# A hybrid layer on one NeuronCore: work between the scans issued by a running account of engine times, in place of fixed credits

## The chip, the cores and the metric

The kernel runs on one core of one Trainium2 chip. The metric is the device time of one execution in microseconds, lower is better. Each engine of the core (PE for matmuls, DVE for vector work, ACT for activations, POOL for general elementwise work, SP for issuing DMAs) runs its own list of instructions in the order in which the program issued them; engines wait for each other through semaphores. PEld is the loading of weights on the PE.

## The reference, cut to what matters

The input is x of shape 4 x 1024 x 128 in float32. Four blocks follow each other, each with a residual:

```python
x = x + attention(layernorm(x))            # 16 heads of 8; a window of 32 and every 64th position
x = x + mlp(layernorm(x))                  # 128 -> 512 -> 512 -> 128, weights of +1 and -1
x = x + mamba(layernorm(x))                # see below; it adds its own residual as well
x = x + mlp(layernorm(x))
```

The change concerns the third block and the two MLPs beside it. The core of the third block, for E = 256 channels and N = 16 states per channel:

```python
u2 = silu(conv(u) + conv_b)                # depthwise, 4 taps
dt = softplus(dt_lo @ W_dt + b_dt)
def step(h, inp):                          # over the 1024 positions
    dA = exp(dt_t[..., None] * A)
    h = dA * h + (dt_t * u_t)[..., None] * B_t[:, None, :]
    y_t = einsum('ben,bn->be', h, C_t)
y = (y + u2 * D_param) * silu(z)
out = y @ W_out
```

## The kernel before, in words

**Stages.** Attention comes first, in a software pipeline of its own (lines 208 to 590), until about 250 us. Then the first MLP tiles and what the first scan needs are issued by turns until about 321 us. Then come the scans (`scans`, L1059), until about 884 us, with all the rest of the layer woven between them. A tail follows: the last part of the third block's output and its MLP.

**The scans.** A part is one batch element (4) and one half of the sequence (2 x 512 positions): 8 parts in a fixed order. A unit is one part and one of the 16 states: 128 units in order. Each unit i has these instructions, and the loop of `scans` writes their order out by hand:

- `drive(i + 2)`, POOL: `db` = `du` (dt times u2) times the row of B, which a DMA on SP's queue spreads over the partitions (`bs`, `load_b`). Three buffers of `db`.
- `decay(i + 1, h)`, ACT: `da` = exp(dt times A) for each half h of the channels. One tile `da` for each half, with two buffers in PSUM in all, so that `da` of the next unit can only be written when the scan of this unit has read its own.
- two scans, DVE: `hs` from `da` and `db`, one for each half of the channels, with `carry` as the start in the second half of the sequence; in the first half of the sequence ACT copies the last column to `carry`.
- `pcc`, PE: the row of C spread over the partitions by a matmul. One buffer: it can be written when the last unit's `hc` has read it.
- `hc`, DVE: `hs` times `pcc`. Six buffers, shared with some of the MLP's hidden tiles.
- `fold(i)`, POOL: adds `hc` of two neighbouring units, one half of the channels at a time. On POOL it stands ahead of `drive(i + 2)`, and on even i it waits for `hc` of unit i - 1.
- `total(i)`, PE: adds the folded `hc` into `pys` by a matmul with the identity. `gated(i)`, DVE: once in a part and half, `gate` times `pys`.

**The work between.** Everything else is a set of generators (`Work`, L625), which yield a `Piece` (L598) ahead of each small group of instructions: how many PSUM banks the group takes, how many microseconds it costs on which engine (`pe`, `ve`, `sc`, `gp`), whether it empties banks (`evict`), whether it is `urgent`, whether it is a `lump` (two activations with a table load on each side). The generators are: `mamba_pre_half` (L905) for each part (matmuls `pz`, `pc`, `px`, `pd`; activations `gate`, `u2`, `dt`; POOL `du`), `mamba_norm` (L850; `mxn`, `mxnT`, the statistics `rs_z` on POOL), `mamba_out` (L994; `pmo`), and two lanes of `mlp` (L682; `fxn`, `fxnT`, `pf`, `h1`, `pg`, `h2`, `pfo`). Three banks (`SPARE`, L1157) are for them all.

**What sets their order.** The loop of `scans` offers two places in each unit. At each, `evictions()` (L1170) issues every piece that empties banks, whatever it costs, save that lumps wait for the second place; then `pieces()` (L1180) gives each engine half of a fixed credit per unit (`RATES`, L1159: PE 2.9, DVE 1.2, ACT 2.4, POOL 1.2 us) and issues pieces until the credit is spent. The first place lies between `decay(i + 1, 0)` and `decay(i + 1, 1)`, so that what it puts on ACT stands between the two `da` of a unit. `ready` (L1200) issues pieces by force when a unit needs a part that isn't prepared. After the last scan the rest is issued in the order of the list, with `mamba_out_own(B - 1)` (L1020) put at its head.

Of the kernel before, what the change touches and what calls it, by code (L numbers as in the profile page):

```python
# [43 lines left out]
def hybrid_kernel(ctx: ExitStack, tc: tile.TileContext, x, Wq, Wk, Wv, Wo, ln_g, ln_b, W_in, conv_w,  # L44
# [108 lines left out]
    def ln_sums(src, name, soon=False):  # L153

        n = src.shape[1]
        st = small.tile([P, n, 6], F32, tag="st", name=f"st_{name}")
        mv = small.tile([P, n, 2], F32, tag="mv", name=f"mv_{name}")
        if among_scans[0] and not soon:

            for i in range(n):  # L160
                if i % 2 == 0:
                    yield Piece(sc=0.9)
                sc.activation(waste, src[:, i, :], AF.Identity, accum_out=mv[:, i, 0:1])
            yield Piece(gp=0.2)
            gp.tensor_scalar_mul(st[:, :, 0], mv[:, :, 0], -1.0 / C)
            yield Piece()
            for i in range(n):
                if i % 2 == 0:
                    yield Piece(sc=0.9)
                sc.activation(waste, src[:, i, :], AF.Square, bias=st[:, i, 0:1], accum_out=mv[:, i, 1:2])  # L170
            yield Piece(gp=0.2)
            gp.tensor_scalar_mul(mv, mv, 1.0 / C)
            return mv
        for i in range(n):
            if i % 2 == 0:
                yield Piece(ve=0.9)
            ve.bn_stats(st[:, i, :], src[:, i, :])
            ve.bn_aggr(mv[:, i, :], st[:, i, :])
        return mv
# [423 lines left out]


# [20 lines left out]
    class Work:  # L625


        def __init__(self, pieces):
            self.pieces = pieces
            self.held = 0  # L630
            self.next = next(pieces, None)

        def run(self):
            self.held = self.next.banks + (0 if self.next.evict else self.held)
            self.next = next(self.pieces, None)
# [46 lines left out]
    def mlp(u, tiles, split, pool, lane, own=None, soon=False, hasty=False, stats=None):  # L682
# [11 lines left out]
        def empty(dsts, srcs, relu):  # L694


            n = len(srcs)
            yield Piece(n if split else 0, evict=True, sc=0.6 * n, same=soon or hasty)
            for dst, bk in zip(dsts, srcs):
                if relu:  # L700
                    sc.activation(dst[:, 0], bk, AF.Relu)
                else:
                    sc.copy(dst[:, 0], bk)
            if split:
                yield evict(ve=0.7 * n)
                for dst, bk in zip(dsts, srcs):
                    high = dst[:, 0].bitcast(F32)
                    if relu:
                        ve.scalar_tensor_tensor(dst[:, 1], bk, 0.0, high, ALU.max, ALU.subtract)
                    else:  # L710
                        ve.tensor_sub(dst[:, 1], bk, high)
# [3 lines left out]
        yield Piece(sc=1.7)  # L715
        xn = fx.tile([P, nt, C], F32, name=f"fxn{u}", tag=f"fxn{lane}", bufs=1)
        ln_apply(xn, tiles, stats[:, 0], stats[:, 1])
        yield fill(1.2)
# [5 lines left out]
        for f0 in (0, 2):  # L724
            yield fill(1.0 if split else 1.8, 2, ready=(lambda: own or h1_free[0]) if f0 == 0 else None)
            if f0 == 0:
                if own:
                    h1 = own(u)
                else:
                    h1 = pool.tile([P, 4, 2, cols], kind, name=f"h1{u}", tag="h1")  # L730
                    h1 = [h1[:, f] for f in range(4)]
                    h1_free[0] = False
                h2 = pool.tile([P, 4, cols], F32, name=f"h2{u}", tag=f"h2{lane}")
            pf = [bank(f"pf{u}_{f0 + f}")[:, :cols] for f in range(2)]
            for f in range(2):
                w = wt(w0[:, (f0 + f) * P : (f0 + f + 1) * P])
                for s in range(parts):
                    te.matmul(pf[f], w, xnT[:, s], start=s == 0, stop=s == parts - 1)
            yield from empty(h1[f0 : f0 + 2], pf, True)
        for f0 in (0, 2):  # L740
            yield fill(2.0 if split else 1.8, 2)
            pg = [bank(f"pg{u}_{f0 + f}")[:, :cols] for f in range(2)]
            for f in range(2):
                for i in range(4):
                    if (i == 0 and f) or (i == 2 and not split):
                        yield more(2.0 if split else 1.8)
                    w = wt(w1[:, i, (f0 + f) * P : (f0 + f + 1) * P])
                    for s in range(parts):
                        te.matmul(pg[f], w, h1[i][:, s], start=i + s == 0, stop=i == 3 and s == parts - 1)
            yield evict(sc=1.2)  # L750
            for f in range(2):
                sc.activation(h2[:, f0 + f], pg[f], AF.Relu)
# [13 lines left out]
        yield evict(ve=0.75)  # L766
# [83 lines left out]
    def mamba_norm(bp, c):  # L850
# [10 lines left out]
        yield Piece(gp=2.2)  # L861
# [10 lines left out]
        yield Piece(sc=1.7)  # L872
# [9 lines left out]
        yield fill(1.2)  # L882
# [3 lines left out]
        yield Piece(sc=1.7, same=True)  # L886
# [18 lines left out]
    def mamba_pre_half(b, f):  # L905
# [16 lines left out]

        u2 = m2.tile([P, NH, CH], F32, name=f"u2{v}", tag="u2", bufs=3)
        for h in range(NH):
            for k in range(DC):
                if h + k == 0:
                    yield fill(1.8, 2, urgent=late)
                    pc = [bank(f"pc{v}_{h}") for h in range(NH)]
                elif k % 2 == 0:
                    yield Piece(pe=1.8, urgent=late)  # L930
                te.matmul(
                    pc[h], w_conv[:, k, h * P : (h + 1) * P], xnT[:, k : k + CH], start=k == 0, stop=k == DC - 1
                )
# [11 lines left out]
        yield fill(1.8, urgent=True)  # L945
# [7 lines left out]
        if not place:  # L953
# [3 lines left out]
            yield Piece(-1, urgent=True, sc=1.8)  # L957
# [17 lines left out]
        yield fill(1.8, 2, urgent=True)  # L975
# [18 lines left out]
    def mamba_out(bp, f):  # L994
# [3 lines left out]
        for q in range(HALF):  # L998
            yield fill(2.2)
            po = bank(f"pmo{bp}_{f}{q}")  # L1000
            for b2 in range(2):
                if b2:
                    yield more(2.2)
# [8 lines left out]
            yield evict(ve=0.75)  # L1012
# [7 lines left out]
    def mamba_out_own(b):  # L1020
# [6 lines left out]
        yield fill(1.7)  # L1027
        po = bank(f"pmo{b}_own")
        for g in range(4):
            if g == 2:  # L1030
                yield more(1.7)
# [27 lines left out]
    def scans(wide, ready):  # L1059
# [48 lines left out]
        def gated(i):  # L1108
# [3 lines left out]
            if not 0 <= k <= last:  # L1112
                return
            b, f, n = units[k]
            if n == N - 2:
                gate = mamba_pre[b, f][0]
                ve.tensor_mul(gate[:, h], gate[:, h], py.pop((b, f, h)))
                if h == NH - 1:
                    fed.add(("g", b, f))

        for i in range(3):
            load_b(i)
        for i in range(2):
            drive(i)
        for h in range(NH):
            decay(0, h)
        for i, (b, f, n) in enumerate(units):
            now[0] = i
            load_b(i + 3)
            fold(i)  # L1130
            drive(i + 2)
            pc = wide.tile([P, CH], F32, name=f"pcc{i}", tag="pcc")
            te.matmul(pc, spread[: 6 * N, n, :], mamba_pre[b, f][4], start=True, stop=True)
            hs = m2.tile([P, NH, CH], F32, name=f"hs{i}", tag="hs")
            db = dbs.pop(i)
            for h in range(NH):
                first = carry[b % 2][:, h, n : n + 1] if f else 0.0
                ve.tensor_tensor_scan(hs[:, h], das.pop((i, h)), db[:, h], first, ALU.mult, ALU.add)
            decay(i + 1, 0)
            evictions(lumps=False)  # L1140
            pieces()
# [3 lines left out]
            gated(i)  # L1145
            hss[i] = m2.tile([P, NH, CH], F32, name=f"hc{i}", tag="hc", bufs=6)
            ve.tensor_tensor(hss[i], hs, pc.unsqueeze(1).to_broadcast([P, NH, CH]), ALU.mult)
            total(i)
            evictions()
            pieces()  # L1150
# [6 lines left out]
    SPARE = 3  # L1157

    RATES = {"pe": 2.9, "ve": 1.2, "sc": 2.4, "gp": 1.2}  # L1159
    works = []  # L1160
    owed = dict.fromkeys(RATES, 0.0)

    def issue(w):
        for k, us in w.next.us.items():
            owed[k] -= us
        w.run()

    emptied = set()

    def evictions(lumps=True):  # L1170
        emptied.clear()
        for w in works:
            while w.next is not None and w.next.evict and (lumps or not w.next.lump):
                hasty = w.next.same
                issue(w)
                emptied.add(w)
                if w.held and not hasty:
                    break

    def pieces(forced=False):  # L1180


        for k, rate in RATES.items():
            owed[k] = min(max(owed[k], -2 * rate) + (0 if forced else rate / 2), rate / 2)
        left = SPARE - sum(w.held for w in works)
        for w in works:

            moved = w in emptied and now[0] < len(units) - 10
            while w.may() and not w.next.evict and w.next.banks <= left:
                if moved and not w.next.same and not (forced and w in emptied):  # L1190
                    break
                if not (forced or w.next.hurries()) and any(us and owed[k] <= 0 for k, us in w.next.us.items()):
                    break
                left -= w.next.banks
                issue(w)
                moved = True
            if forced and moved:
                break

    def ready(*part):  # L1200
        while part not in prepared:
            evictions()
            pieces(forced=True)
# [50 lines left out]
    with banks(SPARE), tc.tile_pool(name="wide", bufs=1, space=PSUM) as wide:  # L1254
# [12 lines left out]
        while any(w.next for w in works):  # L1267
            evictions()
            pieces(forced=True)
# [35 lines left out]
```

## Time and profile before

| what | us |
|---|---|
| median of 3 runs (lowest, highest) | 920.89 (917.93, 923.53) |
| the profiled execution's own time | 918.99 |
| its span, first to last instruction | 917.2 |
| first scan begins, last `hc` ends | 323.82, 884.47 |
| between these two: busy DVE, POOL, PE, ACT | 506.90, 507.93, 477.20, 406.60 |
| busy in the whole span: DVE, POOL, PE, ACT | 756.8, 747.2, 753.5, 592.3 |

The page's fifth part and the groups of instructions give for each kind its count, busy time, mean duration in ns and the idle time of its engine just before it, with what ended that. Nearly all instructions pass through one helper and so carry its line, L57: they are told apart by their tiles, which are named "out<-in". The waits give who waited for whom, in us, times and the longest. In the timeline a row starts with its start and its length in us. PEclk is the share of the full clock that was granted to the PE.

### The profile page before, as it was taken

The page shows a single profiled execution, that of the slowest core. Times are in us where ns is not written, and L with a number is a line of the kernel's source. Part 1 is how long each engine was busy: PE and PEld are TensorE (multiplying, and loading weights), DVE is VectorE, ACT ScalarE, POOL GpSimd, SP SyncE. Part 2 cuts the span into 40 slices and gives each one's busy share as a digit, 9 for nine tenths or more (in the row PEclk, how much of TensorE's full clock was granted, in tenths as well). Part 3 has the DMA queues.
Part 4 walks back from the last instruction along what each step waited for, and adds up shares of the span by engine and source line. Part 5 has one row for each costly group of instructions (what it writes and reads, how often), then busy time and mean ns, then how long its engine had stood idle before and what let it go on. Part 6 is the DMA issues. An engine that isn't in the chain of part 4 may idle for free.

```text
span 917.2 us, 15260 instructions
## 1 busy us (share of the span) xinstructions
PE 753.5 (82%) x5642; PEld 450.8 (49%) x5642; DVE 756.8 (83%) x1014; ACT 592.3 (65%) x1299; POOL 747.2 (81%) x580
## 2 busy tenths in 40 slices
PE   5797768875688978797789888969989889788897
PEld 2455435543466534442355444425455446455567
DVE  6699898999643279889799888897999999999862
ACT  4775537753345587889866777977777865654523
POOL 6699996999533188999988988999989999989730
PEclk9999769987589999897999997977999899899899
DMA  4633213330000121112111111211121222122001
GB/s 129 125 71 70 45 32 69 73 66 2 32 17 1 35 76 57 43 69 71 67 50 69 46 69 49 69 55 62 63 77 58 81 70 65 62 81 81 24 1 35
DMA packets 47163, 53.09 MB, mean 58 GB/s; under 512 B 4825, under 2 KB 38401, under 8 KB 47089
## 3 DMA queue, kind: packets, MB, share of 16 engines
q1 hardware_dynamic: 45920, 51.59, 19.9%
q8 instruction: 44, 0.72, 0.3%
q0 software_dynamic: 608, 0.27, 0.2%
q10 hardware_dynamic: 560, 0.26, 0.1%
q14 instruction: 31, 0.25, 0.1%
HBM read 45.82 MB, written 4.46 MB: 55 GB/s over the span
## 4 chain that ended last, share of the span: by engine, by line
DVE 32%; PE 26%; POOL 20%; ACT 12%; issue 8%; DMA 2%; SPq 0%; DVEq 0%; POOLq 0%; ACTq 0%
DVE hs L57 14%; POOL db L57 5%; DVE hc L57 5%; PE pga L57 4%; DVE S L57 4%; PE pys L57 4%; POOL prod L57 3%; POOL hc L57 3%; POOL prodv L57 3%; PE pc L57 3%; ACT da L57 2%; ACT L57 2%; PE pgb L57 2%; PE pfoa L57 2%; DVE or L57 2%
## 5 line engine op out<-in xcount | busy, mean ns | idle before, releaser
L57 POOL TENSOR_TENSOR db<-du,bs 128x1024 f32<-128x1024 f32 x128 | 302.6, 2365 | 0.7 <-DMA bs<-bd 0.7
L57 ACT ACTIVATE da<-dt,a_t 128x512 f32<-128x512 f32 x256 | 175.4, 687 | 127.2 <-DVE hs L57 126.6
L57 POOL TENSOR_TENSOR hc<-hc,hc 128x512 f32<-128x512 f32 x128 | 163.1, 1275 | 43.0 <-DVE hc L57 42.8
L57 DVE TENSOR_TENSOR hc<-hs,pcc 128x1024 f32<-128x1024 f32 x128 | 156.0, 1219 | 28.8 <-PE pcc L57 21.1
L57 DVE TENSOR_TENSOR_SCAN hs<-da,db 128x512 f32<-128x512 f32 x128 | 149.4, 1207 | 14.6 <-POOL db L57 7.3
L57 DVE TENSOR_TENSOR_SCAN hs<-da,carry,db 128x512 f32<-128x512 f32 x128 | 157.1, 1268 | 4.6 <-ACT da L57 4.6
L57 PE MATMUL pys<-hc,ident 128*128 128x512 f32 x256 | 147.1, 660 | 0.8 <-POOL hc L57 0.8
L57 PE MATMUL pcc<-bc,spread 96*128 96x512 bf16 x128 | 52.3, 409 | 35.7 <-DVE hc L57 34.8
L57 PEld LDWEIGHTS pys<-hc,ident 128*128 128x128 f32 x256 | 51.3, 210 | 51.7 <-issue 33.3
L57 PE MATMUL pga<-h1a,w 128*128 128x512 f32 x256 | 72.2, 431 | 2.5 <-ACT gate L57 1.8
L57 POOL TENSOR_TENSOR prod<-kv,qs 128x128 f32<-128x128 f32 (+14 forms) x30 | 71.0, 2368 | 3.2 <-DVE or L57 3.0
L57 POOL TENSOR_TENSOR prodv<-vS,E 128x128 f32<-128x128 f32 (+14 forms) x30 | 69.4, 2312 | 5.1 <-ACT E L57 4.8
L57 PE MATMUL pc<-mxnT,w_conv 128*128 128x512 f32 x128 | 61.8, 609 | 5.9 <-ACT gate L57 5.9
L57 ACT ACT_TABLE_LOAD x48 | 61.6, 1283 | 3.5 <-issue 2.6
L57 PEld LDWEIGHTS pga<-h1a,w 128*128 128x128 f32 x256 | 49.7, 197 | 27.8 <-issue 7.5
L57 PE MATMUL pgb<-h1b,w 128*128 128x512 f32 x192 | 59.0, 453 | 4.4 <-DVE fxnTc L57 3.1
L57 ACT ACTIVATE E<-S 128x512 f32<-128x512 f32 (+15 forms) x62 | 26.5, 473 | 52.1 <-DVE S L57 51.9
L57 PE MATMUL ps<-kx,qT 64*32 64x256 f32 x1008 | 46.8, 440 | 8.3 <-DVE S L57 5.8
L57 PEld LDWEIGHTS pgb<-h1b,w 128*128 128x128 f32 x192 | 38.2, 200 | 26.6 <-issue 7.4
L57 PE MATMUL py<-woT,oT 128*128 128x128 f32 x64 | 17.9, 368 | 39.0 <-ACT oT L57 38.7
L57 POOL TENSOR_TENSOR ep<-ep,eo 128x512 f32<-128x512 f32 x32 | 40.9, 1278 | 9.7 <-ACT ep L57 8.5
L57 ACT COPY ep<-pt 128x512 f32<-128x512 f32 x32 | 18.8, 586 | 38.8 <-DVE eo L57 36.1
(223 smaller groups left out, 1551.8 us busy)
## 6 DMA issues: line engine op xcount, KB each, us to landing
bs<-bd SPq DMA_DIRECT2D x64, 512.0 KB
vr<-vd SPq DMA_DIRECT2D x32, 256.0 KB
vd<-kv SPq DMA_DIRECT2D x8, 256.0 KB
x<-in_L_attn_a_x_dram SPq DMA_DIRECT2D x15, 128.0 KB
kx<-kT SPq DMA_DIRECT2D x104, 16.0 KB
out_dram<-x SPq DMA_DIRECT2D x12, 128.0 KB
taps<-in_L_attn_b_conv_w_dram SPq DMA_DIRECT2D x1, 512.0 KB
k1s<-in_L_ffn_k_dram SPq DMA_DIRECT2D x1, 256.0 KB
```

What stands on the lines that cost most here:

```text
L57: ins = getattr(self.engine, name)(*args, **kwargs)
```

## The change

Each engine gets a clock of the program's own (`times`), which `spend` moves on by a stated duration when an instruction is issued, starting no earlier than what it waits for. The loop of `scans` keeps it for its own instructions with durations written out in it. `ends` works out from it when a piece would be done, and whether the DVE would have to wait for it. At both places of a unit `pieces` issues whatever would be done by a deadline per engine, counted from the DVE's time; a piece in which the DVE would wait is held back. Pieces that empty banks are no longer exempt. The first place now lies after both `decay(i + 1, ·)`. Urgent is what a part needs that is 8 units away or less. The two lanes are taken in the order of which has issued fewer pieces. After the last scan, the piece that would be done first comes first. Stated durations are changed a little (ACT's statistics up, transposes from 1.2 to 0.65). The instructions themselves are the same.

```diff
-    RATES = {"pe": 2.9, "ve": 1.2, "sc": 2.4, "gp": 1.2}
+    times = dict(pe=0.0, ve=0.0, sc=0.0, gp=0.0)
...
+    def spend(engine, us, *others):
+        times[engine] = max(times[engine], *others, 0.0) + us
+        return times[engine]
+
+    def ends(w):
+        t, found, waits = w.since, {}, False
+        for k, us in w.next.us.items():
+            waits = waits or (k == "ve" and t > max(times[k], found.get(k, 0.0)) + 0.1)
+            t = found[k] = max(times[k], t) + us
+        return found, waits
...
+    def pieces(until=None):
+        for w in works[:-2] + sorted(works[-2:], key=lambda w: w.count):
+            moved = False
+            while w.may():
+                p = w.next
+                if not p.evict and p.banks > SPARE - sum(v.held for v in works):
+                    break
+                if until and p.us and (moved or not p.hurries()):
+                    found, waits = ends(w)
+                    spare_time = 0.8 if p.lump else 0.0
+                    if waits or any(t > until[k] + spare_time for k, t in found.items()):
+                        break
+                issue(w)
+                moved = moved or bool(p.us)
+                if not until:
+                    return
...
             decay(i + 1, 0)
-            evictions(lumps=False)
-            pieces()
             if f == 0:
                 sc.copy(carry[b % 2][:, :, n : n + 1], hs[:, :, CH - 1 :])
             decay(i + 1, 1)
-            gated(i)
+            t = times["ve"]
+            pieces(dict(pe=t + 2.0, ve=t + 1.5, sc=t + 4.2, gp=t + 6.2))
+            if gated(i):
+                spend("ve", 0.68, *after(("sum", i - 1)))
...
             total(i)
-            evictions()
-            pieces()
+            done["sum", i] = spend("pe", 0.9, *after(("fold", i - 1)))
+            t = times["ve"]
+            pieces(dict(pe=t + 1.7, ve=t + 1.5, sc=t + 3.0, gp=t + 5.0))
...
+        def hurry():
+            return now[0] >= place * PER - 8
...
         while any(w.next for w in works):
-            evictions()
-            pieces(forced=True)
+            able = [
+                w for w in works if w.may() and (w.next.evict or w.next.banks <= SPARE - sum(v.held for v in works))
+            ]
+            issue(min(able, key=lambda w: max(ends(w)[0].values(), default=w.since)))
```

## The prediction

> **What bounds the kernel now.** I read the stretch of the scans first (a table of busy times by stage), then the waits in it, then the timeline where waits are long.
>
> ```profile
> core 0: us, PE busy (x) PEld busy (x) DVE busy (x) ACT busy (x) POOL busy (x), PEclk, DMA share, GB/s
> 323.82:393.97 70.15, 56.45 (x196) 30.98 (x195) 62.41 (x70) 57.30 (x112) 63.38 (x47) 0.93 0.18 61
> 393.97:466.78 72.81, 57.21 (x145) 25.65 (x144) 61.27 (x59) 59.35 (x132) 68.23 (x55) 0.86 0.19 66
> ...
> 811.33:884.47 73.14, 61.88 (x248) 39.65 (x247) 68.42 (x72) 38.50 (x78) 56.38 (x40) 0.91 0.16 51
> sum 560.65, PE 477.20 PEld 265.52 DVE 506.90 ACT 406.60 POOL 507.93; mean PE 59.65 PEld 33.19 DVE 63.36 ACT 50.83 POOL 63.49
> ```
>
> Each row is one part of 16 units. The scans last 560.65 us, 4.38 a unit; DVE works 506.90 of it and POOL 507.93. Two engines are 90% busy, none is full. Which of them paces is told by the waits:
>
> ```profile
> engine line waited for: us in total, times, longest us
> ACT da L57 <- DVE hs L57: 126.6, 108, 4.0
> POOL hc L57 <- DVE hc L57: 37.9, 31, 4.0
> PE pcc L57 <- DVE hc L57: 34.8, 33, 3.1
> DVE hc L57 <- PE pcc L57: 21.1, 22, 3.5
> DVE hs L57 <- ACT da L57: 11.8, 11, 2.0
> DVE hs L57 <- POOL db L57: 7.3, 2, 7.0
> DVE fxnTa L57 <- ACT fxnTa L57: 5.1, 2, 2.7
> ```
>
> POOL, ACT and PE wait for the DVE. The DVE waits for PE's `pcc` 21.1 us, for `da` 11.8, and for POOL only 0.3 (the other 7.0 us are the start, ahead of the stretch). So DVE paces, and its idle time, 560.65 - 506.90 = 53.75 us, is what there is to win: `pcc` 21.1, `da` 11.8, `db` 0.3, its own evictions (`fxnT`, `h1`, `x`, nine kinds of wait together) 12.5, and 8.0 in gaps with no named releaser. A `da` wait as it looks on ACT:
>
> ```profile
> 621.61 0.69 ACT L57 ACTIVATE da<-dt,a_t 128x512 f32<-128x512 f32 x1
> 622.23 0.57 ACT L57 CAST bc<-px 32x512 bf16<-32x512 f32 x1
> 622.71 0.67 ACT L57 ACTIVATE da<-dt,a_t 128x512 f32<-128x512 f32 x1
> 623.33 1.63 ACT L57 ACTIVATE x<-x,rs_z 128x128 f32<-128x128 f32 x4
> 624.87 0.18 ACT L57 COPY carry<-hs 128x2 f32<-128x2 f32 x1
> 624.95 0.68 ACT L57 ACTIVATE da<-dt,a_t 128x512 f32<-128x512 f32 x1
> ```
>
> A `bc` and four `x` stand just ahead of the second `da` of a unit; so, too, did four `mxn` before 621.61, where the DVE lost 1.39 us.
>
> **What the Trainium skill says.** "Perfetto Trace Analysis", Optimization Strategy: take the most-contended engine, find the gaps between its slices and what blocks them; that is the way above, and this trace adds that of two equally busy engines the waits must choose. "TensorE: Matmul & The Clock Gate", Architectural detail: ACT and DVE are strict FIFO and PE only pulls weight loads ahead; the trace agrees, `da` waits behind `bc`. "ScalarE: Activation LUTs", What ACT_TABLE_LOAD costs: 1283 ns, and about 1380 of drain; the trace has 1283 for each of 48, and no such drain (load at 625.64, `dt` at 626.94).
>
> **The change, part by part**, by the order of instructions in the two built programs beside the durations above. The instructions are the same; all else is order.
>
> (1) *Both `da` first.* In the new order nothing stands between a unit's two `da` but the `carry` copy, which waits for the same scan as the second `da`. Extra ACT work comes behind them and can only delay the next unit's first `da`. From the end of a unit's scans, a lump there gives 0.70 + 0.18 for `da` and `carry`, 1.28 + 1.27 + 1.28 for the lump, 0.69 for the next `da`: 5.4 us. The DVE asks for it after `hc`, two scans, `hc`: 1.22 + 2.33 + 1.22 = 4.8. A lump costs 0.6 where the DVE has no extra work, and none where it has one (0.68 or more). There are 22 lumps (8 `gate`, 7 `u2`, 7 `dt`); I count about half: 6 us stay of 11.8. Bounds: 0 and 22 x 0.6 = 13.
>
> (2) *Deadlines for PE.* PE may be given work until 2.0 us past the scans, and 1.7 past `hc`; `pcc` (0.38) then has the next two scans (2.33) as cover. The cover fails where PE is slower than stated: eight `pga` matmuls are stated 1.9 and took 3.53 us at 565.59, with a granted clock of 0.70. The waits of 2.85 and 3.45 us lie in stretches at 0.70 and 0.68; these 6.3 stay, and one urgent `px` is put ahead of `pcc` 59: 7 us stay of 21.1. Bounds: 2 and 15.
>
> (3) *No eviction in which DVE would wait.* Held until the account says the data is there. Durations were nearly right, so 4 of 12.5 stay (1 to 8). Gaps of 8.0 stay.
>
> (4) *What is late next: POOL.* It has 507.93 us of work and its order is bound: fold, `db`. From the end of an `hc` it needs 1.27 + 2.36 = 3.6 us for `db`, while DVE asks for it after two units, 2 x 3.6 = 7.2: a slack of 3.6 us, which POOL can't widen, as the fold waits for `hc`. In quiet units DVE takes 2.33 + 1.22 = 3.55 and POOL 1.275 + 2.365 = 3.64, so a lag is made good only while DVE has extra work. The new order puts extras of 1.29 (`du`) to 2.7 us (`rs_z`) close together four times: near units 10 to 13, 40 to 44 (7.2 us in five units), 58 to 63, 68 to 71. At some 2 us beyond the slack each, the DVE now waits for `db`: 9 us in place of 0.3. This wait isn't in the trace of before; bounds 0 (the DVE's extras cover all) and 20 (POOL paces: 507.93 plus what it still waits). `du` of the fifth part now comes just ahead of `db` 64; its `dt` is done about 2.7 us after scan 61, its fold at 2.5, and `db` 64 at 7.7 where scan 64 asks at 8.5: nothing. On SP's queue the row of B for that part is written some units later than before, ahead of the same loads; `db` has waited for it only 0.7 us in all, and I count none.
>
> Sum: 7 + 6 + 4 + 8 + 9 = 34 idle in place of 53.75, a gain of 19.75. One DVE instruction more falls before the last `hc` (the last but one `x`, 0.75).
>
> (5) *The tail.* Before, after the last `hc`:
>
> ```profile
> 883.37 2.43 PE L57 MATMUL pgc<-h1c,w 128*128 128x512 f32 x8
> 885.64 2.74 PE L57 MATMUL pys<-hc,ident 128*128 128x512 f32 x6
> 888.38 0.46 PE L57 MATMUL pmo_own<-w_out,gate 128*128 128x128 f32 x2
> ...
> 892.96 3.84 PE L57 MATMUL pfoc<-w,h2c 128*128 128x128 f32 x32
> 896.63 1.95 PE L57 MATMUL pfob<-w,h2b 128*128 128x128 f32 x16
> 899.52 0.63 PE L57 MATMUL ftpc<-ident,fxnc 128*128 128x128 f32 x4 [0.94 <-DVE x L57]
> ```
>
> Counted from the start of that `hc` (883.25), `pmo_own` ends at 9.7 and `ftpc`, on which all the rest hangs, starts at 16.3. In the new order three groups of eight `pgc` (2.1 each) stand between the last `pys` and the end of `pmo_own`; one takes the time in which the PE waited for `gate`, so `pmo_own` ends at about 15.4. `pfob` is done earlier; then follow `pfoc` 3.84 and the DVE's 0.75 with its latency: `ftpc` at about 20.3, 4.0 us later. Bounds 2 and 6.
>
> Net: 19.75 - 0.75 - 4.0 = 15.0 us. From the profiled execution's 918.99 (span 917.2 and 1.8 around it) that is 904.0; it stood 1.9 below the median of 920.89, so the forecast is 920.89 - 15 = 905.9, taken as 905.5.
>
> **Rivals.** *A, nearly all stalls go.* `pcc` 3, `da` 3, `db` 2, evictions 2, gaps 8: 18 idle, so 53.75 - 18 - 4.75 = 31: 890. For it: PE, ACT and POOL wait long for DVE, there is room. Against it: POOL has 508 us of work. *B, POOL takes over*: `db` 20, net 4: 917. For it: 3.64 against 3.55 in quiet units. Against it: 37.9 us of POOL's waiting. *C, slower: PE becomes the bound*, as the account takes its work at full clock. PE works 477.20 us at a mean clock of 0.91, or 434 at full clock; I leave it 25 us of waits that no order takes away (half of the 34.8 for `hc`, and the 7.7 of `px` for `w`). At clock c the scans last 434 / c + 25. With the 4.75 us of the tail and the moved instruction, it decides from 434 / c + 25 = 556, c = 0.82; at 0.80 they last 568, and the kernel 568 - 560.65 + 4.75 = 12 more: 933. For it: parts at 0.86, stretches at 0.7. Against it: no part has gone below 0.86. That the change doesn't do what it says is ruled out by the built order, in which the pairs of `da` stand together throughout.
>
> **How the numbers follow.** The forecast 0.50 (its own range 897 to 913), A 0.20, B 0.17, C 0.13. The range for 8 in 10 leaves out C and the lower part of A: 887 to 921. About 0.5% (4.6 us) is what a measurement here can tell from no change: faster is the forecast, A and a quarter of B, 0.74; same is most of B, 0.13; slower is C, 0.13.
>
> **What would show it.** After: DVE's waits for `pcc` about 7 us, for `da` about 6, for `db` about 9, its evictions about 4; POOL's wait for `hc` well below 37.9; first scan to last `hc` about 541 us; `ftpc` about 20 us after the last `hc` begins. Wrong if `pcc` waits stay near 21 (the PE's durations are what fails), if `db` passes 15 (B), or if the stretch's clock falls to 0.82 (C).

## The result, and the profile after

The changed kernel takes 931.65 us (930.24 to 932.9, 4 runs) where the kernel before takes 919.7 (917.93 to 923.53, 4 runs). The ratio is 1.0124, 95% interval 1.0086 to 1.0161: it is 1.2% slower. The forecast was 905.5, and its range ended at 921.

The stretch from the first scan to the end of the last `hc`, in the table of busy times of the changed kernel:

```profile
core 0: us, PE busy (x) PEld busy (x) DVE busy (x) ACT busy (x) POOL busy (x), PEclk, DMA share, GB/s
324.24:893.75 569.51, 474.53 (x1697) 265.98 (x1695) 505.00 (x494) 409.66 (x843) 507.69 (x372) 0.91 0.18 61
```

The scans last 569.51 us, 8.9 more than before. What is behind them (929.4 - 893.75 = 35.65 against 917.2 - 884.47 = 32.73) takes 2.9 more, and they start 0.4 later: 12.2 in all, which is the growth of the span. Every engine works as long as before to within some 3 us (0.8%) and the clock of this stretch is the same 0.91, so no engine has become slower or got more to do. What grew is the DVE's idle time: 569.51 - 505.00 = 64.5 us against 53.75. The waits of the same stretch say where:

```profile
engine line waited for: us in total, times, longest us
ACT da L57 <- DVE hs L57: 89.8, 85, 3.9
DVE hc L57 <- PE pcc L57: 47.4, 28, 5.5
...
POOL hc L57 <- DVE hc L57: 24.0, 18, 3.6
...
DVE hs L57 <- POOL db L57: 9.4, 3, 7.1
```

The wait for `pcc`, which was to fall from 21.1 to 7, has more than doubled, to 47.4. `db` is 2.3 (7.1 of the 9.4 are the start), and `da`, by the list of the DVE alone, 1.6 in place of 11.8. The DVE's other instructions wait 6.7 in place of 12.5 (2.0 of it is `gated`, which waits for `pys`), and 6.5 stay without a named releaser.

**What stands before a late `pcc`.** The third longest comes in unit 30 (5.16 us; the two longer ones are 5.49 and 5.25). First ACT's timeline of the changed kernel (start, duration, what, and in brackets the idle time before it), then PE's, then the `hc` on the DVE:

```profile
453.61 0.69 ACT L57 ACTIVATE da<-dt,a_t 128x512 f32<-128x512 f32 x1
454.31 1.28 ACT L57 ACT_TABLE_LOAD   x1
455.60 1.09 ACT L57 ACTIVATE gate<-pz 128x512 f32<-128x512 f32 x2
456.71 1.28 ACT L57 ACT_TABLE_LOAD   x1
```

```profile
451.73 1.79 PE L57 MATMUL pga<-h1a,w 128*128 128x512 f32 x7
456.25 3.78 PE L57 MATMUL pga<-h1a,w 128*128 128x512 f32 x8 [2.73 <-ACT gate L57]
459.83 1.91 PE L57 MATMUL pys<-hc,ident 128*128 128x512 f32 x2
461.53 0.63 PE L57 MATMUL pcc<-bc,spread 96*128 96x512 bf16 x1
```

```profile
462.21 1.22 DVE L57 TENSOR_TENSOR hc<-hs,pcc 128x1024 f32<-128x1024 f32 x1 [5.16 <-PE pcc L57]
```

Eight `pga` need a bank that `pz` holds until the `gate` lump has read it. (A piece that takes banks and fills them by PE, like these `pga`, is called a fill below.) The lump starts behind two decays at 454.31 and frees its first bank about 456.2. The `pga` stand at the head of PE's queue all that time, 2.73 us idle, and `pys` and the 0.4 us of `pcc` stand behind them. Then PE runs at half speed:

```profile
452.24:455.65 3.41, 1.28 (x6) 0.71 (x4) 3.31 (x4) 2.81 (x5) 3.41 (x4) 1.00 0.02 8
455.65:459.07 3.42, 2.82 (x7) 2.26 (x8) 1.39 (x2) 3.39 (x6) 3.42 (x3) 0.50 0.31 96
459.07:462.48 3.41, 3.41 (x7) 1.74 (x6) 0.27 (x1) 1.44 (x3) 3.41 (x3) 0.50 0.17 58
462.48:465.89 3.41, 3.41 (x10) 1.44 (x9) 3.31 (x4) 0.87 (x3) 1.56 (x1) 1.00 0.12 49
```

The columns are those of the first fence above; the clock is the number behind the POOL column. It is 0.50 from 455.65 to 462.48. The eight `pga` take 3.78 us in it, against some 2.2 in most groups of eight; `pys` takes 1.91 and `pcc` 0.63, where they took 1.02 and 0.38 at full clock (448.90 and 448.68 of this trace). So a pause of 2.73 and a loss of some 2.7 more become 5.16 us of the DVE.

**Why the program lets that fill through.** `Work.run` lowers `held` when the piece that empties a bank is *issued*, not when it is done; `pieces` asks only whether `SPARE` minus the held banks suffices, and `ends` adds up engine times but knows no bank. As soon as the lump is issued, a fill in the same call of `pieces` may take its banks, and the account books its start up to the lump's 3.8 us too early. In the built order 18 of the 22 lumps go out at the first place of a unit and 15 of these are followed by a fill at the same place. In the kernel before no lump goes out at the first place. What PE itself had waited for just before each wait on `pcc` tells more: nine of the 28 stand behind a fill that waited over 0.5 us for a lump (`gate`, `u` or `dt`), in units 1, 2, 7, 11, 30, 39, 59, 65 and 88, together 23.7 us. In the built order each of the nine has one of the 15 fills in the unit just before it. In the kernel before there are four such, 4.9 us. The difference, 18.8, is most of the 26.3 by which the wait grew.

### The profile page after: what moved, and what is told of

The parts are those of the page before. It is cut to its first block, busy times and chain, and to the rows that moved or that the text cites. A ratio compares the mean times of both kernels' runs of the same rounds, so it can differ in the third digit from the quotient of the medians.

```text
span 929.4 us, 15270 instructions
## 1 busy us (share of the span) xinstructions
PE 757.4 (81%) x5642; PEld 454.3 (49%) x5642; DVE 754.0 (81%) x1014; ACT 596.7 (64%) x1299; POOL 746.9 (80%) x580
## 3 DMA queue, kind: packets, MB, share of 16 engines
q1 hardware_dynamic: 45920, 51.59, 19.6%
## 4 chain that ended last, share of the span: by engine, by line
DVE 33%; PE 29%; ACT 14%; POOL 13%; issue 8%; DMA 2%; SPq 0%; DVEq 0%; POOLq 0%; ACTq 0%
DVE hs L57 16%; PE pys L57 5%; PE pga L57 5%; DVE S L57 4%; ACT da L57 3%; DVE hc L57 3%; ACT L57 3%; POOL prod L57 3%; POOL prodv L57 3%; PE pc L57 3%; POOL db L57 2%; PE pgb L57 2%; DVE or L57 2%; POOL hc L57 2%; PE pfoa L57 2%
## 5 line engine op out<-in xcount | busy, mean ns | idle before, releaser
L57 DVE TENSOR_TENSOR hc<-hs,pcc 128x1024 f32<-128x1024 f32 x128 | 155.8, 1217 | 53.3 <-PE pcc L57 47.4
L57 PE MATMUL pc<-mxnT,w_conv 128*128 128x512 f32 x128 | 59.2, 593 | 1.6 <-ACT h2a L57 1.5
L57 POOL TENSOR_TENSOR du<-dt,u 128x512 f32<-128x512 f32 x16 | 20.3, 1285 | 29.0 <-ACT dt L57 29.0
```

What stands on the lines that cost most here:

```text
L57: ins = getattr(self.engine, name)(*args, **kwargs)
```

## The experiments

The theory (1): fills that are let through behind a lump. The first rival (2): the account books PE's own work too short. Further rivals: the moved place, the late urgency, the order of the tail. Each ratio is to runs of the kernel before that were made beside that run; their medians lie between 918.9 and 922.9, so the ratios compare better across rows than the times. The pieces of the span are those of each profiled execution, waits are the DVE's inside the scans.

| run | us | ratio to before (95%) | scans | behind them | waits `pcc` | waits `da` |
|---|---|---|---|---|---|---|
| before | 919.7 | 1 | 560.7 | 32.7 | 21.1 | 11.8 |
| after | 931.65 | 1.0124 (1.0086, 1.0161) | 569.5 | 35.7 | 47.4 | 1.6 |
| banks_known | 952.56 | 1.035 (1.0322, 1.0379) | 563.2 | 64.5 | 44.0 | 6.9 |
| after_no_tables | 911.9 | 0.9919 (0.9892, 0.9946) | 551.0 | 35.6 | 29.2 | 0.3 |
| before_no_tables | 908.48 | 0.9875 (0.9846, 0.9904) | 549.8 | 32.7 | 18.4 | 4.7 |
| before_place_moved | 934.09 | 1.0157 (1.0128, 1.0187) | 574.2 | 32.7 | 27.9 | 10.4 |
| after_place_back | 920.64 | 1.0006 (0.9994, 1.0018) | 561.4 | 34.6 | 30.8 | 12.1 |
| pe_scaled | 951.23 | 1.0318 (1.0284, 1.0351) | 570.1 | 54.1 | 53.9 | 6.4 |
| hurry17 | 944.31 | 1.0253 (1.0219, 1.0287) | 586.1 | 34.7 | 46.7 | 0.9 |
| tail_list | 931.27 | 1.0116 (1.0091, 1.014) | 570.2 | 36.7 | 46.5 | 0.9 |
| after_sc_drawn | 924.94 | 1.0056 (1.003, 1.0081) | 558.4 | 38.5 | 21.6 | 2.7 |
| place_back_sc16 | 926.02 | 1.005 (1.0027, 1.0073) | 555.0 | 45.1 | 29.4 | 6.4 |
| both_places | 921.72 | 1.0036 (1.0018, 1.0055) | 562.1 | 34.7 | 33.6 | 1.7 |
| bank_next | 909.69 | 0.9902 (0.9869, 0.9935) | 545.7 | 34.5 | 23.7 | 2.0 |
| lumps_second | 926.12 | 1.0072 (1.005, 1.0094) | 556.1 | 46.1 | 32.4 | 0.6 |
| both_lumps_second | 918.54 | 0.9987 (0.9972, 1.0002) | 551.7 | 39.6 | 28.7 | 1.5 |
| bank_next_back | 916.5 | 0.9922 (0.9886, 0.9959) | 552.1 | 39.6 | 19.6 | 11.2 |

### banks_known: the account is told when banks come free

```diff
+    freed = [0.0] * SPARE
...
         t, found, waits = w.since, {}, False
+        if w.next.banks > 0 and not w.next.evict and w.next.banks <= len(freed):
+            t = max([t, *freed[: w.next.banks]])
...
+        held = w.held
         w.run()
+        if w.held > held:
+            del freed[: w.held - held]
+        else:
+            freed.extend([w.since] * (held - w.held))
```

> The changed kernel, with one thing added to its account: it keeps the times at which the five spare PSUM banks come free (the end, by the account, of the eviction that empties each) and starts a fill no earlier than its banks. Nothing that is computed changes. Theory 1 (a fill that was let through stands at the head of TensorE's queue until ScalarE has emptied a bank by a lump, and the short matmul of the scan, pcc, stands behind it): VectorE's waits on pcc fall from 47.4 us towards the 21 to 28 of the kernel before, and the time comes to 910 to 917. Theory 2 (the account books TensorE's own operations too short, since they take twice as long after a pause): the waits stay over 40 and the time within 4 us of 931.

(There are three spare banks, not five.) It takes 952.56: as a mend it fails, and neither theory foresaw it. The scans are 6.3 us shorter than in the changed kernel, but one wait of 18.9 us stands in unit 93, where a part had to be finished by force, and 64.5 us are left behind the scans. The DVE did 497.6 us of work inside them, not 505.0. A fill that can't be done by its deadline is now held back unless it is urgent, so less work is done beside the scans. This run judges the mend and not the theory: waits behind a lump are down to two, 6.0 us, but less was issued as well, so this alone can't be put down to the missing fills.

### after_no_tables and before_no_tables: shorter lumps

```diff
-            sc.activation(gate[:, h], pz[h], AF.Silu)
+            sc.activation(gate[:, h], pz[h], AF.Relu)
```

and the same for `u` (Silu) and `dt` (Softplus), in both kernels.

> The changed kernel with Relu in place of Silu and Softplus in the gate, u and dt lumps, so that no table is loaded: this leaves those functions out of what is computed; the order of the instructions is the same. A lump on ScalarE is some 2.6 us shorter. Theory 1 (fills stand behind banks that a lump frees): the nine waits behind a lump, 23.7 us in the changed kernel, fall below 6 and the time falls by 17 to 30, to 902 to 915. Theory 2 (TensorE's own durations): the waits on pcc stay over 38 and the time falls by less than 10.

> The kernel before with the same Relu in place of Silu and Softplus in the three lumps, which leaves those functions out of what is computed, in the order of before. It is the base for the run above. Theory 1: before has only 4.9 us of waits behind a lump and some 12 us of waits for late decays, of which a shorter lump takes a part; the time falls by 5 to 15, to 905 to 914, and the changed kernel without tables is then no slower than this one. Theory 2: the changed kernel stays about 10 us slower than this one.

The changed kernel gains 19.8 us, the kernel before 10.4. Of the 12 us between the two, 3.4 stay. In the changed kernel the wait on `pcc` falls by 18.2, the part behind lumps from 23.7 to 6.5. The order and PE's work are the same as in the changed kernel, so theory 2 (waits over 38) is refuted as the main cause. Theory 1 isn't met to the letter: 6.5 is not under 6, and after_no_tables stays 3.4 us slower than before_no_tables. Some of the wait stays: `pcc` is 29.2 here and 18.4 there.

### before_place_moved: one part of the change alone

```diff
-            evictions(lumps=False)
-            pieces()
             if f == 0:
                 sc.copy(carry[b % 2][:, :, n : n + 1], hs[:, :, CH - 1 :])
             decay(i + 1, 1)
+            evictions(lumps=False)
+            pieces()
             gated(i)
```

> The kernel before with one part of the change alone: the first of the two places for other work in a unit stands behind both decays of the next unit instead of ahead of the second, the fixed credits are kept. If the order around the decays is worth what the prediction's first step says, the 11.8 us of waits on a late decay fall under 4 and the time by 5 to 10, to 910 to 914. If moving the place costs as much as it gives (the evictions on VectorE and ScalarE come later, so banks come free later), the waits on pcc rise over 26 and the time stays within 3 us of 919.7.

It costs 15 us, more than either expectation. The scans are 13.5 us longer; of the idle time, `pcc` has 6.8 more, the DVE's own pieces, which wait for ACT or PE, 7.8 more, and the waits on `da` are still 10.4. Pieces on ACT now queue behind the second `da`, which waits for the second scan. The waits on `da` come in two kinds, and the move reaches only one. In the kernel before, only 4.0 of the 11.8 us stand ahead of a unit's second half scan, and here these are gone; 7.8 stand ahead of the first half scan, and here they are 10.4. For example, at 441.52 a `gate` lump of the second place and an `mxnT` stand ahead of *both* decays of a unit, and the DVE waits 2.86 us for them. In the changed kernel this kind is 1.6. The moved place alone doesn't do that; the rest of the change, the account with its deadlines, does. Which part of it isn't shown.

### after_place_back, after_sc_drawn, place_back_sc16, both_places: place or deadline

after_place_back moves the first place back between the decays, with `sc=t + 2.4`; place_back_sc16 is the same with 1.6.

```diff
+            t = times["ve"]
+            pieces(dict(pe=t + 2.0, ve=t + 1.5, sc=t + 2.4, gp=t + 6.2))
             if f == 0:
                 sc.copy(carry[b % 2][:, :, n : n + 1], hs[:, :, CH - 1 :])
             decay(i + 1, 1)
...
-            t = times["ve"]
-            pieces(dict(pe=t + 2.0, ve=t + 1.5, sc=t + 4.2, gp=t + 6.2))
```

> The changed kernel with the first place for other work put back between the two decays of the next unit, as it was before, and ScalarE's deadline there drawn in from 2.4 to the second decay (it was 4.2 behind it); the account and all other deadlines stay. Moving this place alone cost the kernel before 15 us. If the place is the cause of the loss (ScalarE stands on a decay that still waits for a scan, and the evictions queue behind it, so VectorE's own pieces and the banks come late), the time falls to 914 to 922. If the account is the cause (fills let through ahead of banks that lumps free), the waits on pcc stay over 38 us and the time stays within 5 us of 931.

With the place put back the loss is gone (920.64, ratio 1.0006). `da` is at 12.1 again, 9.5 of it ahead of second half scans, and `pcc` at 30.8, with 4.3 of it behind lumps. But place and deadline were changed together, and this decides which lumps go out where: in this order none goes out at the first place. Hence the next three.

after_sc_drawn leaves the place and changes `sc=t + 4.2` to `sc=t + 3.2`.

> The changed kernel, the first place left behind both decays, with ScalarE's deadline there drawn in from 4.2 to 3.2 us behind the second half scan, which is when ScalarE was to be done with pieces and second decay in the run with the place put back. It tells the place from the deadline. If the place itself costs (evictions queue behind a decay that waits for a scan), the time stays at 927 to 936 and the waits on pcc over 38 us. If it was the looser deadline that let lumps in ahead of evictions, it falls to 916 to 923 and the waits under 33.

> The changed kernel with the first place put back between the two decays and ScalarE's deadline there at 1.6 us instead of 2.4. With 2.4 VectorE waited 12.1 us for late decays, in 18 waits of some 0.7. If these come from pieces let in at this place, they fall under 5 us and the time by 4 to 8, to 913 to 917. If less is then let through and banks come free later, the waits on pcc rise by as much (over 36 us) and the time stays within 3 us of 920.6.

both_places leaves the place and adds one between the decays:

```diff
             decay(i + 1, 0)
             done["da", i + 1, 0] = spend("sc", 0.65, *after(("hs", i, 0)))
+            t = times["ve"]
+            pieces(dict(pe=t + 2.0, ve=t + 1.5, sc=t + 1.5, gp=t + 6.2))
```

> The changed kernel with a further place for other work between the two decays, where ScalarE's deadline is 1.5 us behind the second half scan, and the first place behind both decays kept. If the loss comes from evictions that stand behind the second decay, the waits on pcc fall from 47 to under 33 us while those on decays stay under 5, and the time comes to 908 to 917, under the kernel before. If the three places let more fills through than banks are emptied, the waits on pcc stay over 40 and the time over 925.

The drawn-in deadline alone takes the wait on `pcc` to 21.6 (2.7 behind lumps) and the time to 924.94, 2 us above what was expected of it. It, too, leaves no lump at the first place, so it doesn't separate the deadline from the place of the lumps. Its scans are even shorter than those of the kernel before, but the DVE's other instructions wait 19.4 us in them and 38.5 us are left behind them. place_back_sc16 makes the scans 555.0 and leaves 45.1, and ends at 926.02: neither of its two expectations. both_places, which keeps 4.2, has 21 of 22 lumps at the place behind both decays and again some 22 us of its waits behind lumps; it ends at 921.72 and not at the 908 to 917 of the first expectation. So what a variant gains in the scans is partly given back behind them.

### pe_scaled, hurry17, tail_list: the rivals

```diff
-            t = found[k] = max(times[k], t) + us
+            t = found[k] = max(times[k], t) + us * (1.25 if k == "pe" else 1.0)
```

> The changed kernel with TensorE's durations in the account multiplied by 1.25, nothing else. If the account's error is that TensorE's operations are booked too short (groups of 1.9 us that took 3.8 after a pause), the waits on pcc fall from 47 to under 30 and the time to 912 to 918. If the error is the banks that a lump on ScalarE has still to free, longer bookings don't see them: waits over 38, time 926 to 936.

```diff
-            return now[0] >= place * PER - 8
+            return now[0] >= place * PER - 17
```

> The changed kernel in which the pieces on the way to the next stretch of the scan become urgent, and so pass the deadlines, 17 units ahead of it instead of 8. If the late rush ahead of a stretch is a main part (the waits after the 59th and 61st unit, 6.8 us, and the crowding around them), the time falls by 5 to 8, to 923 to 927. If urgent pieces cost by passing the deadlines at all, the waits on pcc rise over 50 us and the time to 933 to 940.

tail_list replaces the choice of the soonest piece in the last loop by `pieces()`.

> The changed kernel in which the work behind the last scan is issued in the order of the list, as before, and not the piece that the account has done soonest; the scans are unchanged. If the order is what made the tail 3.0 us longer, the stretch from the end of the last product of a scan to the end of the program falls from 35.7 to about 32.7 and the time to 928. If it is work left over by the scans, the stretch and the time stay within 1 us.

pe_scaled has waits of 53.9 on `pcc` and 54.1 us left behind the scans: 951.23, slower than either expectation. Booking PE longer holds work back and doesn't help the waits. hurry17 is worse too (944.31), again beyond both expectations: `pcc` stays at 46.7, 32.9 of it behind lumps, and the DVE waits for `pfoa`, `pys` and `pmo`, 17.2 us for these three. tail_list changes nothing (931.27), so the tail isn't longer because of the last loop's order.

### bank_next, lumps_second, both_lumps_second: the fills or the lumps

bank_next lets the banks of a lump count as free only from the next place on, and nothing else:

```diff
+    fresh = [0]
...
     def pieces(until=None):
+        fresh[0] = 0
...
-                if not p.evict and p.banks > SPARE - sum(v.held for v in works):
+                if not p.evict and p.banks > SPARE - fresh[0] - sum(v.held for v in works):
                     break
...
+                held = w.held
                 issue(w)
+                if p.lump:
+                    fresh[0] += held - w.held
```

> The changed kernel, places and deadlines as they are, in which the two banks that a lump empties count as free only from the next place on (the account as it is counts them free as soon as the lump is issued). By its order 17 of the 22 lumps still go out at the first place, but a fill follows one at the same place 6 times instead of 15. If the fills that follow a lump at the first place are the cause, the nine waits behind lumps (23.7 us) fall under 6, those on pcc from 47 to under 32 and the time to 916 to 923. If lumps at the first place cost by themselves (what ScalarE has queued behind them), the time stays at 927 to 935.

lumps_second breaks off at a lump in the first place (`if p.lump and not lumps: break`); both_lumps_second does so in both_places.

> The changed kernel in which no lump is issued at the first place of a unit; places, deadlines and the rest stay, and all 22 lumps go out at the second place (in the changed kernel 18 go out at the first). If lumps at the first place are the cause, the waits on pcc fall from 47 to under 32 and the time to 916 to 923. If the cause is the rest of ScalarE's looser deadline or the place itself, it stays at 927 to 935.

> The changed kernel with a further place for other work between the two decays (with ScalarE's deadline at 1.5 us), and lumps issued only at the last place of a unit. If the two causes are separate (lumps at the place behind both decays; evictions that queue behind the second decay), both are gone: the waits on pcc fall under 28 us, those on decays stay under 5, and the time is 908 to 916, under the kernel before. If what is gained in the scans is left over for the end, the stretch behind the last scan grows over 38 us and the time stays at 918 to 925.

bank_next takes 909.69, 22 us less than the changed kernel and 1.0% less than the kernel before (0.9902, interval 0.9869 to 0.9935). It is the fastest kernel of this study that computes everything. 17 lumps still go out at the first place; what is gone is the fill right behind most of them (6 have one, where it was 15). Its scans and the DVE's waits in them:

```profile
326.92:872.58 545.66, 466.44 (x1706) 262.32 (x1704) 505.37 (x494) 409.92 (x844) 506.05 (x372) 0.93 0.18 64
```

```profile
engine line waited for: us in total, times, longest us
...
DVE hc L57 <- PE pcc L57: 23.7, 21, 3.0
...
DVE hs L57 <- POOL db L57: 2.4, 2, 2.0
```

The wait on `pcc` is halved, 9.2 of it still behind lumps (six waits; under 6 us was expected). The time fell further than the expected 916 to 923. Of the 23.7 us that are gone from `pcc`, 14.5 are waits behind lumps; the other 9.2 come with the order as it changes after each held fill, and their cause isn't shown. The same moment as above, with the same lump at the same time (its `gate` starts at 455.74), on PE and DVE:

```profile
452.25 2.41 PE L57 MATMUL pga<-h1a,w 128*128 128x512 f32 x8
454.98 0.38 PE L57 MATMUL pcc<-bc,spread 96*128 96x512 bf16 x1 [0.32 <-DVE hc L57]
456.39 2.13 PE L57 MATMUL pga<-h1a,w 128*128 128x512 f32 x8 [1.03 <-ACT gate L57]
```

```profile
457.28 1.22 DVE L57 TENSOR_TENSOR hc<-hs,pcc 128x1024 f32<-128x1024 f32 x1
```

The same eight `pga` still wait for `gate`, but `pcc` has gone ahead of them. PE's pause is 1.03 in place of 2.73, the `pga` take 2.13 us, and `hc` starts without a wait.

That lumps at the first place cost by themselves is refuted by bank_next, which keeps 17 of them there. lumps_second shows the other half. Without lumps at the first place the scans are 13.4 us shorter and the waits behind lumps 5.2, though a fill follows 18 of its 21 lumps at the second place. (`pcc` is at 32.4, 46.1 us are left behind the scans, and the time is 926.12, between its two expectations.) So the loss takes both: a lump at the place right behind both decays, and a fill behind it. By the built orders and traces of the other runs with lumps of full length this holds throughout:

| lumps at the place right behind both decays | with a fill behind them | waits on `pcc` behind lumps | runs |
|---|---|---|---|
| 17 to 21 | 14 to 18 | 14.1 to 32.9 us | after, tail_list, both_places, pe_scaled, hurry17 |
| 17 | 5 or 6 | 6.0, 9.2 us | banks_known, bank_next |
| none; 18 to 21 at the last place of a unit, behind `hc` | 14 to 18 | 2.7 to 7.6 us | after_place_back, after_sc_drawn, place_back_sc16, lumps_second, both_lumps_second |

Why a fill behind a lump costs so much less at the second place, no run shows. both_lumps_second has much shorter scans (551.7) and again more behind them (39.6): 918.54, its second expectation.

### bank_next_back: the first step without the fault

The two edits of bank_next and after_place_back together.

> The changed kernel with both edits: the banks that a lump empties count as free from the next place on, and the first place is put back between the two decays (ScalarE's deadline there 2.4). It asks what the moved place, the prediction's first step, is worth once no fill follows a lump. If that step was right by itself, this run has some 10 us of waits on late decays again, which bank_next (2.0 us of them) has not, and takes 915 to 921 against 909.7. If the place between the decays is better by itself and only hid the fault, it takes 900 to 907.

The waits on `da` are back (11.2 against 2.0 in bank_next), those on `pcc` a little lower (19.6 against 23.7, none of it behind lumps). The time is 916.5, within the first expectation, its ratio 0.9922 (0.9886 to 0.9959) beside 0.9902 (0.9869 to 0.9935) for bank_next. The intervals overlap: whether the moved place is worth anything by itself isn't settled.

## Why the prediction was wrong, by its own steps

**Step (2), deadlines for PE, failed**, and with it the sign. It counted 7 us of waits on `pcc`, bounds 2 to 15; there were 47.4. It said that PE may be given work until 2.0 us past the scans, with `pcc` covered by the next two scans, and looked for the error only in PE's durations (clock). But a deadline in the account covers a fill only if the fill can start when the account says. I took "what PE is given" for "what PE can start", although the description of the kernel says that three banks are for all the work and that a lump empties them. The diff shows `held` lowered at issue. The term of the sum that was missing is: 15 fills behind lumps at the first place. Nine of them made `pcc` late by 2.6 us each on average, 23.7 us. bank_next, which takes nine of the 15 away and with them changes the order of what follows, takes 22 us off.

Even with most of the fault gone, in bank_next, `pcc` is 23.7 and not 7; 9.2 of it are still behind lumps. What causes the rest isn't settled; in 11 of the 15 other waits PE has no pause over 0.5 us just before, and booking PE longer (pe_scaled) doesn't mend them.

**Step (1)** gave the right direction (1.6 us of waits on `da`, 6 forecast) for a reason that holds only in part. It treated the 11.8 us as if the pairing of the `da` ended them all, save what lumps cost anew. Only 4.0 of them were waits for a second `da`, and the order alone left 10.4 in before_place_moved. The example misled: `bc` at 622.23 stands ahead of a unit's first `da`, and only the four `x` ahead of the second. The step also took the cost of the move as nothing. In before_place_moved it was 15 us, and the likely payers, by the waits there, are the evictions on ACT that queue behind a second `da` which waits for a scan.

**Step (3)** was near: 6.7 us, or 4.7 without `gated`, forecast 4, bounds 1 to 8. The gaps are 6.5, forecast 8. **Step (4)**: `db` 2.3, forecast 9, inside its bounds; POOL doesn't take over. **Step (5)**: 2.9 us more behind the scans, forecast 4.0; `ftpc` starts 19.15 us after the last `hc` began, forecast 20.3.

With the measured sizes the sum is 47.4 + 1.6 + 6.7 + 6.5 + 2.3 = 64.5 idle in place of 34: 30.5 more, of which step (2) alone is 40.4 and the others give back 9.9. The miss in the span is 27.2 (929.4 against 917.2 - 15.0): the DVE's work fell by 1.9 where it was to grow by 0.75, the tail grew by 1.1 less than forecast, and the scans start 0.4 later.

**Rival C** had the right sign and the wrong mechanism. It needed a clock of 0.82 over the scans; it was 0.91. Its grain of truth is local: in the place shown above the clock fell to 0.50, but after PE had stood idle behind a bank. **Rival B** (POOL) didn't come. The forecast's mechanism, fewer stalls by deadlines, exists: with one edit to the bank count the kernel takes 909.69, inside the range of the prediction, and its scans 545.7 us where 541 were said to show the forecast right. Part of that is luck: its `pcc` is 23.7 where 7 was forecast, and `db` 2.4 where 9 was, and such misses cancel.

## What to carry to other kernels

A schedule made from durations must also know when buffers come free: a matmul that is issued behind a bank still to be read stops everything behind it on PE, and here the short operation that the slowest engine needs was the one that paid. When a late operation is found, ask what stood at the head of its engine's queue and what that waited for, before its duration is blamed. And judge a new order by the whole span: six variants here that hold work back have shorter scans than the changed kernel and leave 2.9 to 28.8 us more for the end.

## What the runs showed of the hardware

PE's clock can fall without a long pause. "TensorE: Matmul & The Clock Gate" of the Trainium skill, Part 1, gives as the condition for half rate an idle window of some 3.4 us, and says that the window runs freely. The half rate agrees: 0.50 granted, and 3.78 us for a group that else takes 2.21. The window agrees too: from 324 to 880 us, in the scans of all 17 traces, the granted clock changes only on a grid of 3.41 us. The table of four windows around the example, further up, is cut along it.

But the window need not be idle. In the first of the four, PE was busy for 1.28 of 3.41 us, 38%, and the next was granted half. In the second it was busy for 2.82 us, 82%, and the half rate stayed; after one that was full the full clock came back. Over the same stretch of all 17 traces, with PE's busy time as the profile gives it, there were 145 windows at full clock in which PE was busy for less than 40%, and all were followed by half rate. Of 1807 that were busy for 65% or more, 22 were. Of 145 windows at half rate with less than 80%, none was followed by the full clock.

So in this kernel the length of one pause doesn't decide. A `pgb` group behind a pause of 3.05 us took 3.78 as well, and after pauses of 1.03 us (bank_next) and 1.83 us (a `pga` group in the kernel before) groups of eight took 2.13. But behind pauses of 2.31 us (a `px` at 583.80 of the changed kernel) and 2.09 us (a `pfoa` at 426.41) the clock stayed at 1.00. What the clock follows, with few exceptions, is how much of a fixed window PE works; between 40% and 65% both outcomes occur.
